# Layer 0's attention by pairs of query tiles, and the norms' inverse root as a power on GpSimd

## The chip, the cores and the metric

The kernel runs on one core of one Trainium2 chip. The core has five engines that run side by side, each with its own queue of instructions in a fixed order: TensorE (PE, matrix products and transposes, with a separate record for its weight loads, PEld), VectorE (DVE), ScalarE (ACT, table functions such as the exponential), GpSimd (POOL) and SyncE (SP, which here issues transfers). They meet through semaphores. TensorE writes into PSUM, eight banks of 128 partitions by 512 numbers in 32 bits; the other data lie in SBUF. The metric is the time on the device in microseconds (us) of one execution, the median of three runs.

## The reference

The input x is [4, 2048, 256] in 32-bit floats: 4 batches of 2048 positions. Two layers are computed, each as

```
xn = layernorm(x)                       # (x - mean) / sqrt(var + 1e-5), over 256
x  = x + mixer(xn) + second(xn)
```

In layer 0 the mixer is a gated linear recurrence along the 2048 positions (two 256x256 gates, then a scan). The second part is an attention of which, for every batch, the 4 most probable of 16 heads are chosen and scaled by gates:

```
dist = softmax(mean_over_positions(x @ Wr + br)); idx = top 4 of dist
Q, K, V = the chosen heads' projections, each [2048, 64], times the gate
attn = softmax(Q K^T / 8) over 2048 keys      # no mask
out  = concat(attn V) @ Wo + bo
```

In layer 1 the mixer is a causal attention with 16 heads of 16, and the second part is a channel mixing with sigmoid and squared relu. Layer 1 is not edited by the change, but its input is layer 0's x through the second norm, and the next batch's first norm is computed during its last part.

Note one property of the code below: the keys of a head are taken in the kernel as two halves of 1024 positions, so that 64-row operands of the two halves can lie in the two row halves of TensorE's array.

## The kernel before

For each batch the kernel does in turn: the first norm and its transposes (for batches after the first this runs beside the end of layer 1 of the batch before), the recurrence's gates and its scan, the choice of heads and the transfer of their weights, the projections of queries, keys and values, layer 0's attention (`attention0`), and layer 1 (`layer1`). The program is written as Python generators that are stepped at chosen places (`steps(stream, count)`), so that pieces of one stage stand in the queues between pieces of another. `in_order` (line 24) fixes that every engine runs its instructions in the order in which the program states them. So the order of the work is written out by hand, and an instruction that waits holds up all that stands behind it on its engine.

**The query tile.** `attention0` runs over the 4 chosen heads k and, for each, over 16 query tiles t of 128 positions. One tile goes through five steps of `Tile0`:

- `scores(j)`, lines 489 to 498, for two blocks j of 512 keys in each of two halves: two matmuls (line 494) with 64 rows each, one per row half of the array, into two banks, and a maximum over each bank on DVE (line 498). A tile has four score banks of 512 keys.
- `exponentials`, line 500: DVE takes the negative maximum `nm` over the four (line 502), and ACT makes four exponentials (line 508), each with its row sum, which appears in the profile as a second instruction, ACTIVATION_READ_ACCUMULATOR. The result is `p`.
- `turn(j)`, line 511: eight transposes of 128x128 (line 518) into two banks, which one DVE and one ACT copy (line 520) bring to `pT`.
- `weigh`, line 523: sixteen matmuls (line 528) of `pT` with the values, with 64 columns each, the two halves of the keys in the two column halves of the array, all accumulating in one bank `acc`; then ACT copies `o` (line 531), and DVE sums the row sums and inverts them, `rc` (lines 533 and 534).
- `project`, line 536: one matmul (line 538) of `o`, whose two halves of 64 rows are the two halves of the keys, with `wo2`, which holds the head's 64 rows of Wo twice; DVE multiplies by `rc` and adds to x (line 540).

A matmul in 32 bits leaves two records in the profile, a transpose one.

**The order in an iteration.** Four tiles are under way at a time. Iteration n states: the scores of the new tile, its exponentials, the projection of the tile three back, `turn(0)` of the last tile, `weigh` of the one before it, `turn(1)` of the last.

**The banks.** Scores have banks 0 to 3 to themselves. Everything else in `attention0` takes turns in banks 4 to 7 (`bank()`). Outside of `attention0` work takes turns in all eight (`own_bank()`), with a counter of its own.

**What stands between the tiles.** In each batch, `background` first finishes the recurrence: the bias is added to its result `y` for each of two halves (line 326, the second of these inside iteration 0), then eight steps, one a tile after tile 0, transpose four blocks of `y` (line 333) and add them to x on DVE (line 335). `rest_of_values` makes the last four value blocks in iteration 0 (lines 442 and 444). Before the head changes, `projecting` makes the next keys (lines 473 and 475) and, at every second head, the next queries (lines 456 and 457), one step a tile. In the last head, `norm.stats` takes the statistics of each finished tile (lines 253 and 254), and `all_blocks` norms each block of four tiles: the root on ACT (line 257), the inverse on DVE (line 261), four rows on DVE (line 268), and two times four transposes (line 274) with a copy by ACT (line 275). `opening` then starts layer 1's projections (lines 639 and 668) while the last tiles drain; layer 1 begins with its scores at line 712.

The first norm of each batch, in `prepared` (line 945), takes the root of all 16 tiles at once.

Of the kernel before, what the change touches and what calls it, by code (L numbers as in the profile page):

```python
# [10 lines left out]
FP = mybir.dt.float32  # L11
BF = mybir.dt.bfloat16
U32 = mybir.dt.uint32
AF = mybir.ActivationFunctionType
# [4 lines left out]
P = 128  # L19
QB = 512  # L20
# [52 lines left out]
def two_layers(ctx: ExitStack, tc: tile.TileContext, x, Wa, Wx, ba, bx, Lam,  # L73
# [36 lines left out]
    turn = {"high": 0, "all": 0}  # L110

    def bank():

        turn["high"] = (turn["high"] + 1) % 4
        return banks[4 + turn["high"]]

    def own_bank():

        turn["all"] = (turn["all"] + 1) % 8
        return banks[turn["all"]]  # L120
# [25 lines left out]
    eps_c = const.tile([P, 1], FP, tag="eps", name="eps_c")  # L146
    POOL.memset(eps_c, EPS)
# [94 lines left out]
    class Norm:  # L242
# [13 lines left out]
        def root(self, t, n):  # L256
            ACT.activation(self.rs[:, t:t + n], self.mv[:, t:t + n, 1:2].rearrange("p n o -> p (n o)"),
                           AF.Sqrt, bias=eps_c)

        def inverse(self, t, n):  # L260
            DVE.reciprocal(self.rs[:, t:t + n], self.rs[:, t:t + n])
# [217 lines left out]
    class Tile0:  # L479


        def __init__(self, b, k, t, qs, kT, v, xt):
            self.name = f"{b}_{k}_{t}"

            self.qT = [qs[(i + k) % 2] for i in range(2)]
            self.k, self.t, self.kT, self.v, self.xt = k, t, kT, v, xt
            self.p = []

        def scores(self, j):
            if j == 0:  # L490
                self.mx = sm.tile([P, 2 * NJ], FP, tag="mx0", name=f"mx0_{self.name}")
            for i in range(2):
                half_ = slice(i * DH, (i + 1) * DH)
                PE.matmul(banks[2 * j + i], lhsT=self.qT[i][half_, self.t * P:(self.t + 1) * P],  # L494
                          rhs=self.kT[half_, j * QB:(j + 1) * QB], start=True, stop=True)
            for i in range(2):
                n = 2 * j + i
                DVE.tensor_reduce(self.mx[:, n:n + 1], banks[n], AX.X, ALU.max)  # L498

        def exponentials(self):  # L500
            nm = sm.tile([P, 1], FP, tag="nm0", name=f"nm0_{self.name}")
            DVE.tensor_reduce(nm, self.mx, AX.X, ALU.max, negate=True)  # L502
            self.sums = sm.tile([P, 2 * NJ], FP, tag="sums", name=f"sums_{self.name}", bufs=4)
            for j in range(NJ):
                p = pex.tile([P, 2, QB], FP, tag="p", name=f"p0_{self.name}_{j}")
                for i in range(2):
                    n = 2 * j + i
                    ACT.activation(p[:, i, :], banks[n], AF.Exp, bias=nm, accum_out=self.sums[:, n:n + 1])  # L508
                self.p.append(p)

        def turn(self, j):

            if j == 0:
                self.pT = half_tile(f"pT_{self.name}").rearrange("p (n q) -> p n q", q=P)
            for i in range(2):
                tr = bank()
                for n in range(4):
                    PE.transpose(tr[:, n * P:(n + 1) * P], self.p[j][:, i, n * P:(n + 1) * P], ident)  # L518
                n0 = 8 * i + 4 * j
                (DVE.tensor_copy if i == 0 else ACT.copy)(self.pT[:, n0:n0 + 4, :],  # L520
                                                          tr.rearrange("p (n q) -> p n q", q=P))

        def weigh(self):
            acc = bank()
            N = NT // 2
            for n in range(N):
                for i in range(2):
                    PE.matmul(acc[i * DH:(i + 1) * DH, 0:P], lhsT=self.v[i][:, n, self.k * DH:(self.k + 1) * DH],  # L528
                              rhs=self.pT[:, 8 * i + n, :], start=(n == 0), stop=(n == N - 1))
            self.o = c1.tile([P, P], FP, tag="o", name=f"o_{self.name}")  # L530
            ACT.copy(self.o, acc[:, 0:P])
            self.rc = sm.tile([P, 1], FP, tag="rc", name=f"rc_{self.name}")
            DVE.tensor_reduce(self.rc, self.sums, AX.X, ALU.add)
            DVE.reciprocal(self.rc, self.rc)  # L534

        def project(self):
            ps = bank()
            PE.matmul(ps[:, 0:D], lhsT=self.o, rhs=wo2[:, self.k, :], start=True, stop=True)  # L538
            xs = rows_of(self.xt, self.t, 1)[:, 0, :]
            DVE.scalar_tensor_tensor(xs, ps[:, 0:D], self.rc, xs, ALU.mult, ALU.add)  # L540

    def attention0(b, xT, xt, ch, recurring, first, v, rest_of_values, norm, opening):


        qk, following = first, None
        background = recurring
        tiles = [None] * 3
        norming = iter(())

        def all_blocks():  # L550

            for q in range(NQ):
                norm.root(4 * q, 4)
                yield
                norm.inverse(4 * q, 4)
                norm.rows(q, 0, 2)
                yield
                yield
                norm.rows(q, 2, 4)
                yield  # L560
                for c in range(2):
                    norm.turn(q, c, ACT.copy)
                    yield
                    yield

        for n in range(NA * NT + 3):
            k, t = divmod(n, NT)
            if t == 0 and 0 < k < NA:
                steps(projecting, 100)
                qk = following  # L570
                following = None
            new = Tile0(b, k, t, *qk, v, xt) if k < NA else None
            last, second, third = tiles
            if t == NT - 6 and k + 1 < NA:
# [6 lines left out]
                projecting = concat(querying, keying)  # L581
            if new:
                new.scores(0)
                new.scores(1)
                if t >= NT - 6 and k + 1 < NA:
                    steps(projecting, 1)
                elif n >= (NA - 1) * NT + 7:
                    if n == (NA - 1) * NT + 7:
                        norming = all_blocks()
                    steps(norming, 1)  # L590
                new.exponentials()
                steps(rest_of_values, 4)
            else:
                steps(norming, 1)
            if n >= NA * NT:
                steps(opening, (1, 2, 1)[n - NA * NT])
            if third:
                third.project()
                if n - 3 >= (NA - 1) * NT:
                    norm.stats(n - 3 - (NA - 1) * NT)  # L600
            steps(norming, 1)
            steps(background, 1)
            if last:
                last.turn(0)
            if second:
                second.weigh()
            if last:
                last.turn(1)
            tiles = [new, last, second]
# [335 lines left out]
    def prepared(b, ready):  # L945
# [6 lines left out]
        def go():  # L952
# [4 lines left out]
            norm.root(0, NT)  # L957
            yield
# [76 lines left out]
```

## Time and profile before

The three runs took 4346.39, 4349.31 and 4352.74 us.

| | |
|---|---|
| median of the runs | 4349.31 us |
| the profiled execution | 4344.38 us |
| its span, first to last instruction | 4342.6 us |
| TensorE busy | 4249.8 us, 98% |
| VectorE busy | 3094.4 us, 71% |
| ScalarE busy | 2818.9 us, 65% |
| GpSimd busy | 1046.4 us, 24% |
| mean granted TensorE clock | 0.994 |
| first batch: first scores of layer 0 to first scores of layer 1 (lines 494 and 712) | 93.5 to 564.9 us |
| second batch: the same | 1168.1 to 1637.9 us |
| ScalarE's table loads for the roots (line 257) | 20, 25.7 us |

How to read it: a row of the timeline is start, duration, engine, line, operation, the tile written and the tiles read, and how many instructions were merged; what stands in brackets is the engine's idle time before it and what ended it. PE's busy time counts matmuls that overlap, so a busy PE isn't PE at its peak; the starts of its groups tell how long a group held it. In the table of stretches, a row has the stretch, its length, then busy time and count for PE, PEld, DVE, ACT and POOL, then PEclk, the granted clock as a part of full speed, and the transfers. Durations of single instructions overlap by some tens of nanoseconds where an engine works on several.

### The profile page before, as it was taken

Reading aid. Unit: us, or ns where it says so; the run is one execution under the profiler, and the core shown is the slowest. Engines: PE = TensorE matmul, PEld = TensorE weight load, DVE = VectorE, ACT = ScalarE, POOL = GpSimd, SP = SyncE. Lnnn points to the kernel's source line nnn. Section 1 sums busy time; section 2 is a strip of 40 time slices with the busy share of each in tenths; the row PEclk is TensorE's granted clock in tenths of the full one; section 3 lists DMA queues with packets and bytes.
Section 4 is the critical chain, followed back from the end, with each engine's and each line's share of the span. In section 5 each row is a group of like instructions: output and inputs, shape, how many; then the busy total and the mean of one; then the engine's idle time right before and its main releaser. Section 6 shows DMA issues by size and latency. Waiting matters only on the chain.

```text
span 4342.6 us, 86379 instructions
## 1 busy us (share of the span) xinstructions
PE 4249.8 (98%) x32994; PEld 2351.9 (54%) x32994; DVE 3094.4 (71%) x7292; ACT 2818.9 (65%) x6516; POOL 1046.4 (24%) x1322
## 2 busy tenths in 40 slices
PE   7999999999999999999999999999999999999999
PEld 4666653334566664333456676433446666643334
DVE  6666768887566677888656676888856667688882
ACT  4565648886555664888655566588765556558874
POOL 0000015544100001554410000255440000026544
PEclk9999999999999999999999999999999999999999
DMA  3000010100100000010000000011000000100000
GB/s 84 1 11 1 4 19 17 18 25 16 26 1 11 1 8 16 17 36 6 19 24 1 11 1 11 14 17 36 7 18 23 1 11 1 21 5 16 17 7 23
DMA packets 70818, 65.79 MB, mean 15 GB/s; under 512 B 37234, under 2 KB 58628, under 8 KB 68868
## 3 DMA queue, kind: packets, MB, share of 16 engines
q1 hardware_dynamic: 66624, 57.19, 6.1%
q8 instruction: 260, 4.26, 0.4%
q10 hardware_dynamic: 3780, 3.07, 0.2%
q14 instruction: 154, 1.26, 0.1%
HBM read 16.70 MB, written 8.39 MB: 6 GB/s over the span
## 4 chain that ended last, share of the span: by engine, by line
PE 90%; DVE 7%; ACT 1%; issue 1%; POOL 1%; DMA 1%; ACTq 0%; SPq 0%; POOLq 0%; DVEq 0%
PE bank L737 14%; PE bank L712 13%; PE bank L748 12%; PE bank L494 10%; PE bank L528 10%; PE bank L518 10%; PE bank L923 4%; PE bank L538 3%; DVE mx L498 3%; PE bank L639 3%; PE bank L290 3%; PE bank L473 1%; PE bank L456 1%; DVE mx L718 1%; PE bank L668 1%; PE bank L911 1%
## 5 line engine op out<-in xcount | busy, mean ns | idle before, releaser
L739 ACT ACTIVATE p<-bank 128x512 f32<-128x512 f32 (+3 forms) x2560 | 1183.0, 540 | 362.2 <-PE bank L737 258.4
L712 PE MATMUL bank<-k,q 32*128 32x512 f32 (+3 forms) x5120 | 1171.3, 577 | 1.8
L718 DVE TENSOR_REDUCE mx<-bank 128x1 f32<-128x512 f32 x1536 | 950.1, 681 | 200.5 <-PE bank L712 199.9
L737 PE MATMUL bank<-q,k 32*128 32x512 f32 (+3 forms) x5120 | 1073.4, 556 | 0.0
L508 ACT ACTIVATE p<-bank,nm 128x512 f32<-128x512 f32 x1024 | 689.2, 686 | 501.4 <-DVE nm L502 501.3
L755 POOL TENSOR_TENSOR o<-o,w 128x512 f32<-128x512 f32 (+3 forms) x576 | 627.4, 1089 | 794.7 <-ACT w L754 790.2
L498 DVE TENSOR_REDUCE mx<-bank 128x1 f32<-128x512 f32 x1024 | 635.8, 683 | 200.0 <-PE bank L494 199.8
L737 PEld LDWEIGHTS bank<-q,k 32*128 32x128 f32 x5120 | 422.0, 184 | 544.8 <-ACT p L739 409.1
L748 PE MATMUL bank<-p,v 128*17 128x512 f32 (+3 forms) x5120 | 601.5, 534 | 21.4 <-ACT p L739 14.3
L715 DVE CUSTOM_DVE_ANT_0 bank<-bank,cmask 128x128 f32<-128x128 f32 (+3 forms) x1024 | 472.5, 521 | 160.9 <-PE bank L712 105.6
L518 PE MATMUL bank<-ident,p 128*128 128x128 f32 x4096 | 549.8, 276 | 10.4 <-DVE x L335 5.1
L712 PEld LDWEIGHTS bank<-k,q 32*128 32x128 f32 x5120 | 459.7, 187 | 141.8 <-DVE mx L718 52.0
L520 DVE COPY pT<-bank 128x512 f32<-128x512 f32 x512 | 350.1, 684 | 248.6 <-PE bank L518 248.6
L494 PE MATMUL bank<-k,q 64*128 64x512 f32 x2048 | 514.5, 617 | 7.1 <-DVE v L444 7.1
L528 PE MATMUL bank<-pT,v 128*64 128x128 f32 x8192 | 503.8, 276 | 9.2 <-DVE x L540 8.5
L518 PEld LDWEIGHTS bank<-ident,p 128*128 128x128 f32 x4096 | 457.6, 141 | 82.0 <-DVE rc L534 22.6
L647 POOL MEMSET q<- 128x2048 f32 x16 | 29.6, 1848 | 1837.7 <-PE bank L528 1837.7
L528 PEld LDWEIGHTS bank<-pT,v 128*64 128x64 f32 x8192 | 441.9, 137 | 54.5 <-issue 34.8
L754 ACT COPY w<-bank 128x512 f32<-128x512 f32 (+3 forms) x576 | 305.3, 530 | 106.2 <-PE bank L748 85.2
L748 PEld LDWEIGHTS bank<-p,v 128*17 128x17 f32 x5120 | 88.8, 95 | 439.8 <-ACT p L739 237.2
L520 ACT COPY pT<-bank 128x512 f32<-128x512 f32 x512 | 309.7, 606 | 19.0 <-PE bank L518 17.7
L742 POOL TENSOR_SCALAR_AFFINE_SELECT p<-p 128x256 f32<-128x256 f32 x512 | 205.4, 413 | 385.4 <-ACT p L739 379.7
(164 smaller groups left out, 3495.3 us busy)
## 6 DMA issues: line engine op xcount, KB each, us to landing
x<-in_L_attn_x_dram SPq DMA_DIRECT2D x20, 512.0 KB
q<-q SPq DMA_DIRECT2D x64, 128.0 KB
vals<-o SPq DMA_DIRECT2D x256, 32.0 KB
out_dram<-x SPq DMA_DIRECT2D x32, 256.0 KB
q<-qp SPq DMA_DIRECT2D x48, 128.0 KB
k<-kp SPq DMA_DIRECT2D x48, 128.0 KB
q<-nmT SPq DMA_DIRECT2D x256, 2.0 KB
q<-qp SPq DMA_DIRECT2D x64, 32.0 KB
```

What stands on the lines that cost most here:

```text
L494: PE.matmul(banks[2 * j + i], lhsT=self.qT[i][half_, self.t * P:(self.t + 1) * P], rhs=self.kT[half_, j * QB:(j + 1) * QB], start=True, st ...
L498: DVE.tensor_reduce(self.mx[:, n:n + 1], banks[n], AX.X, ALU.max)
L508: ACT.activation(p[:, i, :], banks[n], AF.Exp, bias=nm, accum_out=self.sums[:, n:n + 1])
L518: PE.transpose(tr[:, n * P:(n + 1) * P], self.p[j][:, i, n * P:(n + 1) * P], ident)
L520: (DVE.tensor_copy if i == 0 else ACT.copy)(self.pT[:, n0:n0 + 4, :], tr.rearrange("p (n q) -> p n q", q=P))
L528: PE.matmul(acc[i * DH:(i + 1) * DH, 0:P], lhsT=self.v[i][:, n, self.k * DH:(self.k + 1) * DH], rhs=self.pT[:, 8 * i + n, :], start=(n == ...
L712: PE.matmul(s[:, 0:n], lhsT=self.qT[strip(h), self.qs], rhs=self.kT[strip(h), self.ks], start=True, stop=True)
L718: DVE.tensor_reduce(self.mx[:, h, :], s[:, 0:n], AX.X, ALU.max)
L737: PE.matmul(s[:, c0:QB], lhsT=self.kT[strip(h), self.ks], rhs=self.qT[strip(h), self.q0 + c0:self.q0 + QB], start=True, stop=True)
L739: ACT.activation(p[:, h % 2, c0:QB], s[:, c0:QB], AF.Exp, scale=SC1)
L748: PE.matmul(acc[32 * h:32 * h + DH1 + 1, c0:QB], lhsT=self.v[h], rhs=self.p[h // 2][:, h % 2, c0:QB], start=True, stop=True)
L755: POOL.tensor_tensor(self.o[:, c0:QB], self.o[:, c0:QB], w[:, c0:QB], ALU.add)
```

## The change

Layer 0's attention runs over pairs of query tiles, `Pair0`, 8 for a head, with a new order; and the norms no longer take a root on ACT.

- **Weighing and projection.** Both tiles of a pair are weighed together into bank 7, which nothing else in `attention0` uses: each tile has one column half of the array and goes through both halves of its keys. So `o` holds one tile in each 64 rows, it is copied once for the pair, and the projection is one matmul of 64 rows per tile, into two banks.
- **The order.** In an iteration stand: the late transposes of the second tile of the pair before, the projection of the pair before that, the first tile's scores and exponentials, half of the second tile's scores, half of the weighing, the other half of the scores, the other half of the weighing, and the first tile's transposes. The second tile's blocks are taken in the order 1, 0.
- **The banks.** `bank()` goes round banks 0 to 6, and shares its counter with `own_bank()`.
- **The steps between.** `background` and `projecting` are stepped at two places of an iteration, at its start and after the late transposes, both ahead of the first tile's scores; the norm's at four. `all_blocks` does the inverse and all four rows of a block at one step, at an iteration's end, and its first transposes at the next step.
- **The norms.** `root` goes. `inverse` adds eps on DVE and raises to the power -0.5 on GpSimd, with a tile that holds -0.5 as the exponent.

```diff
-    turn = {"high": 0, "all": 0}
+    turn = [0]
+
+    def own_bank():
+
+        turn[0] = (turn[0] + 1) % 8
+        return banks[turn[0]]
 
     def bank():
 
-        turn["high"] = (turn["high"] + 1) % 4
-        return banks[4 + turn["high"]]
...
+        if own_bank() is banks[7]:
+            own_bank()
+        return banks[turn[0]]
...
-        def root(self, t, n):
-            ACT.activation(self.rs[:, t:t + n], self.mv[:, t:t + n, 1:2].rearrange("p n o -> p (n o)"),
-                           AF.Sqrt, bias=eps_c)
-
         def inverse(self, t, n):
-            DVE.reciprocal(self.rs[:, t:t + n], self.rs[:, t:t + n])
+            rs = self.rs[:, t:t + n]
+            DVE.tensor_scalar(rs, self.mv[:, t:t + n, 1:2].rearrange("p n o -> p (n o)"), EPS, None, ALU.add)
+            POOL.tensor_tensor(rs, rs, minus_half[:, 0:n], ALU.pow)
...
+        def turn(self, j):
+
+            self.tr[j] = [bank() for _ in range(2)]
+            for i in range(2):
+                for n in range(4):
+                    PE.transpose(self.tr[j][i][:, n * P:(n + 1) * P], self.p[j][:, i, n * P:(n + 1) * P], ident)
+
+        def keep(self, j, i, copy):
...
+            copy(self.pT[:, n0:n0 + 4, :], self.tr[j][i].rearrange("p (n q) -> p n q", q=P))
+
+        def share(self):
+            self.rc = sm.tile([P, 1], FP, tag="rc", name=f"rc_{self.name}", bufs=6)
             DVE.tensor_reduce(self.rc, self.sums, AX.X, ALU.add)
             DVE.reciprocal(self.rc, self.rc)
...
+        def weigh(self, j):
+            acc, N = banks[7], NT // 4
+            for n in range(N):
+                for h in range(2):
+                    for i, tile_ in enumerate(self.tiles):
+                        PE.matmul(acc[i * DH:(i + 1) * DH, 0:P],
+                                  lhsT=self.v[h][:, N * j + n, self.k * DH:(self.k + 1) * DH],
+                                  rhs=tile_.pT[:, 8 * h + N * j + n, :], start=(j == n == h == 0),
+                                  stop=(j == h == 1 and n == N - 1))
+
+        def weighed(self):
+            self.o = c1.tile([P, P], FP, tag="o", name=f"o_{self.name}")
+            ACT.copy(self.o, banks[7][:, 0:P])
...
         def project(self):
...
+            self.ps = [bank() for _ in range(2)]
+            for i in range(2):
+                half_ = slice(i * DH, (i + 1) * DH)
+                PE.matmul(self.ps[i][:, 0:D], lhsT=self.o[half_, :], rhs=wo2[half_, self.k, :], start=True, stop=True)
...
             for q in range(NQ):
-                norm.root(4 * q, 4)
+                yield
+                yield
                 yield
                 norm.inverse(4 * q, 4)
                 norm.rows(q, 0, 2)
-                yield
-                yield
                 norm.rows(q, 2, 4)
                 yield
                 for c in range(2):
                     norm.turn(q, c, ACT.copy)
                     yield
-                    yield
+                yield
+                yield
...
+            steps(background, 1)
+            steps(projecting, 1)
+            steps(norming, 1)
+            if n >= NA * NP:
+                steps(opening, (2, 2)[n - NA * NP])
+            if before:
+                late = before.tiles[1]
+                late.turn(1)
+                late.turn(0)
+                late.keep(1, 0, DVE.tensor_copy)
+                late.keep(0, 0, DVE.tensor_copy)
+                late.keep(0, 1, ACT.copy)
+                late.keep(1, 1, ACT.copy)
+                for tile_ in before.tiles:
+                    tile_.share()
+            steps(background, 1)
+            steps(projecting, 1)
+            steps(norming, 1)
+            if older:
+                older.project()
+                older.add()
+                if n - 2 >= (NA - 1) * NP:
+                    for t in range(2):
+                        norm.stats(2 * (n - 2 - (NA - 1) * NP) + t)
             if new:
...
+                a.scores(0)
+                a.scores(1)
+                a.exponentials((0, 1))
                 steps(rest_of_values, 4)
...
             steps(norming, 1)
...
+            if new:
+                c.scores(1)
+            if n >= NA * NP:
+                steps(opening, 1)
+            if before:
+                before.weigh(0)
+            if new:
+                c.scores(0)
+                c.exponentials((1, 0))
+            if before:
+                before.weigh(1)
+            if new:
+                a.turn(1)
+                a.turn(0)
+                a.keep(1, 0, DVE.tensor_copy)
+                a.keep(0, 0, DVE.tensor_copy)
+                a.keep(1, 1, ACT.copy)
+            if before:
+                before.weighed()
+            if new:
+                a.keep(0, 1, ACT.copy)
+            steps(norming, 1)
+            older, before = before, new
...
-            norm.root(0, NT)
-            yield
             norm.inverse(0, NT)
```

## The prediction

> **What bounds the kernel now.** I read the page's busy shares and the chain that ended last, then the timeline of plain query tiles in layer 0, then the seams of that stage.
>
> ```profile
> PE 4249.8 (98%) x32994; PEld 2351.9 (54%) x32994; DVE 3094.4 (71%) x7292; ACT 2818.9 (65%) x6516; POOL 1046.4 (24%) x1322
> PE 90%; DVE 7%; ACT 1%; issue 1%; POOL 1%; DMA 1%; ACTq 0%; SPq 0%; POOLq 0%; DVEq 0%
> ```
>
> TensorE (PE) is busy and on the path nearly throughout; lines 494, 518, 528 and 538, layer 0's attention, hold a third of the chain. A gain must shorten PE's own row of work there. One plain tile:
>
> ```profile
> 356.83 1.99 PE L494 MATMUL bank<-k,q 64*128 64x512 f32 x8
> 357.99 2.48 DVE L498 TENSOR_REDUCE mx<-bank 128x1 f32<-128x512 f32 x4 [0.80 <-PE bank L494]
> 358.75 0.70 PE L538 MATMUL bank<-wo,o 128*128 128x256 f32 x2
> 359.29 1.04 PE L518 MATMUL bank<-ident,p 128*128 128x128 f32 x8
> 360.25 1.97 PE L528 MATMUL bank<-pT,v 128*64 128x128 f32 x32
> 360.51 0.16 DVE L502 TENSOR_REDUCE nm<-mx 128x1 f32<-128x4 f32 x1
> 360.58 0.47 DVE L540 SCALAR_TENSOR_TENSOR x<-bank,rc,x 128x256 f32<-128x256 f32 x1
> 360.76 0.69 ACT L508 ACTIVATE p<-bank,nm 128x512 f32<-128x512 f32 x1 [2.43 <-DVE nm L502]
> 360.97 0.68 DVE L520 COPY pT<-bank 128x512 f32<-128x512 f32 x1
> 361.35 0.19 ACT L508 ACTIVATION_READ_ACCUMULATOR p<-bank,nm 128x1 f32 x1
> 362.15 1.09 PE L518 MATMUL bank<-ident,p 128*128 128x128 f32 x8
> 363.17 1.99 PE L494 MATMUL bank<-k,q 64*128 64x512 f32 x8
> ```
>
> From scores to scores is 6.34 us: scores 1.92, projection 0.54, half the transposes 0.96, weighing 1.90, the other half 1.02. Inside a group matmuls start every 0.429 us (512 columns), 0.214 (256) or 0.108 (128), two at once where they lie in different row or column halves (the single records of L494 start in pairs 7 ns apart). So 4 x 0.429 + 2 x 0.214 + 16 x 0.108 + 16 x 0.108 = 5.62 us is streaming. The other 0.72 falls where the array's shape changes (128 rows to 64 rows, to 64 columns, and back): four changes a tile, 0.18 each. VectorE (DVE) needs some 4.5 us of the 6.34, ScalarE (ACT) 4.2. So PE alone sets the pace, and two tiles cost 12.68.
>
> **The pair, at PE's own pace.** Scores, transposes and weighing keep their matmuls (10.37 us a pair). The projection of two tiles was 4 x 0.214 = 0.86; now each tile's `o` fills one row half, two streams run at once, and it is 0.43. Changes of shape fall from eight to five (late transposes, projection and scores, weighing, scores, weighing, transposes): 5 x 0.18 = 0.90. Together 11.70 against 12.68. ACT also loses one 0.30 us copy of `o` a pair, off the path.
>
> **The wait that can eat it.** Seven banks now go round for everything. In the changed program's order, counting seven back: the last scores of the second tile reuse the bank of the first scores of the first tile, so PE waits there for that bank's exponential; weighing, transposes and the next pair stand behind. Let x be the start of the first tile's scores. PE reaches that matmul after 1.72 + 0.86 (six scores), 0.09 + 1.79 (half the weighing) and 0.10 for the change: x+4.56. The exponential: the late tile's second DVE copy starts at x-0.87 (its bank is whole 1.50 after the late transposes begin, x comes 2.37 after), takes 0.60, the four sum instructions 0.52, two additions 0.39 each (360.58 to 360.97): DVE is free at x+1.03, the first scores are readable at x+1.06. Maxima to `nm` 2.52 (357.99 to 360.51), to the exponential 0.25, its accumulator read 0.78 after its start, 0.05 to PE: x+4.66. PE waits 0.10. The other reuses come earlier than PE: the next pair's third scores wait for ACT's last late copy, some 0.15 us ahead. A pair takes 11.8: gain 0.88.
>
> **By stretch, each batch (32 pairs).**
> - Sixteen pairs with nothing beside them: 16 x 0.88 = 14.1.
> - Four with the next head's projections after the recurrence is over (tiles 8.06 and 8.21 before): PE's added work hides the wait: 3.9.
> - The first six pairs. Before, the recurrence's transposes come into the second tile. Now a step stands ahead of the first scores, and its transposes wait for `y`:
>
> ```profile
> 93.50 1.99 PE L494 MATMUL bank<-k,q 64*128 64x512 f32 x8
> 94.03 2.35 DVE L312 TENSOR_TENSOR_SCAN y<-at,y,bt 128x1024 f32<-128x1024 f32 x1
> 96.88 1.28 DVE L326 TENSOR_SCALAR y<-y,added 128x2048 f32<-128x2048 f32 x1
> ```
>
> PE is free at 93.5 and `y` is whole at 98.16: 4.7 us of idle PE. Then DVE does both L326 before the first maxima, the second tile's scores come after 7.1 us of values, and the transposes wait for its exponentials, so the second pair's scores start at 116.5 (third tile before: 108.35). The pairs after it take 12.8, 12.8, 12.3, 15.4, 11.8, against 14.25, 14.40, 14.41, 13.54, 16.42: tiles here took 7.20 because weighing waited for a bank held by L540. Sum: 0.2 us lost. In the second and fourth batch PE already idled to 1168.04 and 3312.03, `y` comes 1.1 later, and 3.4 is won.
> - The last six pairs, with the second norm. Two tiles' statistics (0.56 each, 527.10 to 527.66) stand before the maxima on DVE and push the exponential, and PE, by 1.1. Three times `inverse` and all four rows stand at the end of a pair with their transposes first in the next: copy to x+9.8, addition 0.15, power 0.3, hops 0.2, four rows of 0.34: done x+12.0, where PE arrived at x+9.4: 2.2 us of stall behind 0.43 of work. Three pairs of 12.85 and three of 15.9, 86.3 against 80.2: 6.1 lost.
> - The drain: the last block has the same stall, about 2.3, before had some 1.5 of stalls: 0.8 lost.
>
> Per batch 14.1 + 3.9 - 0.2 - 6.1 - 0.8 = 10.9, twice, and 14.5, twice: 50.8.
>
> **The norms.** Root, its table and the exponential's leave ACT, 39 of 58 table loads:
>
> ```profile
> 523.97 1.28 ACT L257 ACT_TABLE_LOAD   x1
> 525.26 0.30 ACT L257 ACTIVATE rs<-mv,eps_c 128x4 f32<-128x4 f32 x1
> 526.75 1.28 ACT L508 ACT_TABLE_LOAD   x1 [1.19 <-DVE nm L502]
> 528.05 0.69 ACT L508 ACTIVATE p<-bank,nm 128x512 f32<-128x512 f32 x1
> ```
>
> The next activation starts with the load's end, so a root costs 2.57 + 0.30. The Trainium skill (ScalarE: Activation LUTs, What ACT_TABLE_LOAD costs) adds a drain of 1.38 us to each switch; the row shows none, and I take the row: 39 x 1.28 = 50 us of ACT, by the page 104, nearly all beside PE. On the path I count 1 us in each of three layer-1 tails (by the page 2), where PE waits on ACT near 1043: 3. There `pow` stands behind a 1.1 us product on POOL, and DVE's rows move some 3 us, under a 4.65 us idle of DVE. The trace has no power on GpSimd (POOL). Nearest rows: 128x512 in 1270 ns and 128x128 in 453 extrapolate to 0.19 for four columns; above, I bound it by the 1.27 itself. I take 0.3, near the extrapolation; at 1.27, four exposed a batch cost 16 more. The last one stands behind two 1.85 us clearings of strips, whose buffers are free early: hidden by the last pair's weighing and six opening projections. At the start it runs under DVE's wait for L214: nothing.
>
> **The clock.** A new 4.7 us idle of PE stands in each batch.
>
> ```profile
> 3308.00:3312.00 4.00, 0.53 (x3) 0.13 (x1) 3.96 (x4) 0.00 (x0) 0.00 (x0) 1.00 0.00 0
> 3312.00:3324.00 12.00, 11.94 (x46) 8.13 (x48) 5.63 (x9) 5.13 (x11) 0.00 (x0) 0.86 0.00 1
> 1164.00:1168.00 4.00, 0.54 (x3) 0.14 (x1) 3.96 (x4) 0.00 (x0) 0.00 (x0) 1.00 0.00 0
> 1168.00:1180.00 12.00, 11.93 (x57) 8.45 (x58) 7.18 (x11) 5.03 (x11) 0.00 (x0) 1.00 0.01 2
> ```
>
> After PE's 3.5 us idle (second column of times) the clock column fell to 0.86 once of two, and that tile took 10.67 in place of 9.02: 1.65. The skill (TensorE: Matmul & The Clock Gate, The HAM clock gate) says one idle window of about 3.4 us halves the clock: four times 1.65, 5.0 more than now. By the rows, half the gaps: 1.6 more. I take 1.6.
>
> **Sum.** 50.8 + 3 - 1.6 = 52 off this execution's 4344.4 (span 4342.6 and 1.8 around it): 4292; the runs' median, 4349.3, lies 4.9 above it: **4297**.
>
> **Rivals.**
> - *Slower, by the bank wait.* Everything from the sums to the exponential is one chain behind one bank. The 52 us over some 116 pairs are 0.45 each: if the exponential releases the bank 5.1 us after x or later, nothing is left; at 5.4, 35 more are lost net, 4384. For it: latencies of 0.05 to 0.25 in a row, and DVE with 9 of 11.8 us filled. Against it: each link is a row, the slack to zero 0.45.
> - *The projection doesn't pair up, or the changes of shape stay.* 0.4 a pair comes back: 4343, within 0.2%. Against it: the paired starts of L494.
> - *Better.* PE waits nowhere in plain pairs (11.70), and DVE takes most of the norm's stalls: 4260 to 4275.
>
> **Numbers.** Forecast 0.62, its own range 4277 to 4320 (0.15 us a pair is 17; the power at its upper bound 16). Better 0.12; projection 0.10; bank wait 0.16. A measurement of this kernel tells 0.2% (8.7 us) from nothing. Faster 0.62 + 0.12 + half of 0.10 = 0.79; within 0.03; slower 0.18. The range takes in the better case and the projection, 4262 to 4345.
>
> **What would show it.** Plain pairs 11.8 from scores to scores; the two projection matmuls start together; PE's wait for the exponential in the last scores under 0.3; 4.7 us of idle before each batch's first transposes of `y`; a 2 us idle before three blocks of the norm; no root tables; `pow` near 0.3. Pairs above 12.3, or a power over 1.3, would make it wrong.

## The result, and the profile after

The changed kernel takes 4370.0 us (median of 5 runs, 4369.6 to 4372.3) against 4350.1 for the kernel before on the same chip: a ratio of 1.0048, 95% interval 1.0033 to 1.0062. It is slower by half a per cent, where 4297 and a gain were forecast. The profiled execution has a span of 4370.6 us against 4342.6.

The page of the kernel after, its busy shares and the chain that ended last:

```profile
PE 4219.6 (97%) x32994; PEld 2366.8 (54%) x32994; DVE 3127.8 (72%) x7292; ACT 2755.3 (63%) x6329; POOL 1072.1 (25%) x1342
PE 86%; issue 5%; DVE 5%; POOL 1%; ACT 1%; DMA 1%; ACTq 0%; SPq 0%; POOLq 0%; DVEq 0%
```

TensorE does the same work in 30 us less, and ScalarE has lost its tables, yet the span grew by 28: TensorE's share of the chain fell from 90 to 86%. Time went into not being busy. First the plain pair, in the timeline of the kernel after (start us, length us, engine, line, operation):

```profile
355.64 1.24 PE L493 MATMUL bank<-k,q 64*128 64x512 f32 x4
...
362.35 0.70 PE L553 MATMUL bank<-wo,o 64*128 64x256 f32 x4
...
362.89 2.74 PE L493 MATMUL bank<-k,q 64*128 64x512 f32 x12
...
366.75 0.69 ACT L507 ACTIVATE p<-bank,nm 128x512 f32<-128x512 f32 x1 [3.21 <-DVE nm L501]
...
367.46 1.24 PE L493 MATMUL bank<-k,q 64*128 64x512 f32 x4
```

From one last group of scores to the next (355.64 to 367.46) it is 11.82 us. The pair does what was forecast; the loss is elsewhere. The seam with the second norm shows most of it, in the same view (L693 is the clearing of a strip, which sets a buffer of layer 1's queries or keys to a constant):

```profile
523.39 0.16 DVE L259 TENSOR_SCALAR rs<-mv 128x4 f32<-128x4 f32 x1
...
523.63 1.01 POOL L260 TENSOR_TENSOR rs<-rs,minus_half 128x4 f32<-128x4 f32 x1 [29.87 <-DVE rs L259]
524.59 1.80 POOL L693 MEMSET q<- 128x2048 f32 x1
524.67 4.57 DVE L267 TENSOR_SCALAR xn<-x,mv,rs 128x256 f32<-128x256 f32 x4 [1.12 <-POOL rs L260]
526.33 1.80 POOL L693 MEMSET k<- 128x2048 f32 x1
...
528.42 1.35 PE L273 MATMUL bank<-ident,xn 128*128 128x128 f32 x4 [5.31 <-DVE xn L267]
...
529.56 3.31 PE L685 MATMUL bank<-xT,wq 128*128 128x512 f32 x4
...
532.71 1.88 PE L685 MATMUL bank<-xT,wk 128*128 128x512 f32 x4
...
550.54 4.83 DVE L267 TENSOR_SCALAR xn<-x,mv,rs 128x256 f32<-128x256 f32 x4 [1.12 <-POOL rs L260]
...
552.90 0.47 PE L273 MATMUL bank<-ident,xn 128*128 128x128 f32 x1 [3.76 <-DVE xn L267]
...
554.79 1.11 PE L273 MATMUL bank<-ident,xn 128*128 128x128 f32 x3 [1.41 <-DVE xn L267]
```

Three things are to be read here. The power takes 1.01 us, and VectorE waits 1.12 for it. The four rows of L267 take 4.57 us in place of some 1.4, exactly while GpSimd clears two strips. And after TensorE's idle of 5.31 us its next four matmuls take 3.31 us, where four of the same size take 1.88 a little later: half clock. At the last block (550.54) the rows meet two more clearings and take 4.83 us, and TensorE idles 3.76 and 1.41.

The windows view of the kernel after (stretch, its length, busy time and count on PE, PEld, DVE, ACT, POOL, then the granted clock) at a batch's start and at the norm's first block:

```profile
94.70:98.90 4.20, 0.00 (x0) 0.00 (x0) 4.16 (x4) 0.20 (x1) 0.00 (x0) 1.00 0.00 0
98.90:105.70 6.80, 6.27 (x16) 3.17 (x17) 4.96 (x8) 0.00 (x0) 0.00 (x0) 0.50 0.01 2
461.20:463.30 2.10, 0.00 (x0) 0.01 (x1) 0.97 (x4) 1.13 (x4) 1.01 (x1) 1.00 0.00 0
463.30:467.70 4.40, 4.38 (x20) 3.91 (x21) 1.96 (x5) 0.59 (x1) 0.00 (x0) 0.61 0.00 2
```

The second stretch is wholly at a clock of 0.50; in the fourth, 0.61 is the mean of 3.4 us at 0.50 (464.17 to 467.58 in the trace's clock record) and the rest at 1.00. In that record every batch has 27 us of it in layer 0, after five idles: 4.7 us before the transposes of `y`, 2.1 us at each of the first two blocks of the norm, 5.3 and 3.8 + 1.4 us at its last two.

Why the clearings run just then is in the waits (engine and line that waited, for whom, us in all, times, longest). Of the kernel before:

```profile
POOL q L647 <- PE bank L528: 1837.7, 8, 498.2
```

and of the kernel after:

```profile
POOL rs L260 <- DVE rs L259: 1936.1, 16, 431.9
```

Before, GpSimd stood at the clearings of layer 1's strips and ran them when their buffers came free. The rows of the norm were nearly or wholly done by then, and kept their 0.7 us for two (timeline of the kernel before):

```profile
500.63 0.73 DVE L268 TENSOR_SCALAR xn<-x,mv,rs 128x256 f32<-128x256 f32 x2
...
501.14 1.97 POOL L647 MEMSET q<- 128x2048 f32 x1 [498.18 <-PE bank L528]
...
507.43 0.70 DVE L268 TENSOR_SCALAR xn<-x,mv,rs 128x256 f32<-128x256 f32 x2
...
508.32 1.81 POOL L647 MEMSET k<- 128x2048 f32 x1 [5.21 <-PE bank L528]
```

Now GpSimd stands at the power. The clearings are queued behind it, their buffers are free by then (the view of the kernel after lists no wait of theirs), and they start the moment the power ends. That moment is also when VectorE's rows start.

### The profile page after: what moved, and what is told of

The parts are those of the page before. It is cut to its first block, busy times and chain, and to the rows that moved or that the text cites. A ratio compares the mean times of both kernels' runs of the same rounds, so it can differ in the third digit from the quotient of the medians.

```text
span 4370.6 us, 86287 instructions
## 1 busy us (share of the span) xinstructions
PE 4219.6 (97%) x32994; PEld 2366.8 (54%) x32994; DVE 3127.8 (72%) x7292; ACT 2755.3 (63%) x6329; POOL 1072.1 (25%) x1342
## 4 chain that ended last, share of the span: by engine, by line
PE 86%; issue 5%; DVE 5%; POOL 1%; ACT 1%; DMA 1%; ACTq 0%; SPq 0%; POOLq 0%; DVEq 0%
PE bank L783 14%; PE bank L758 14%; PE bank L794 12%; PE bank L493 10%; PE bank L515 10%; PE bank L540 10%; PE bank L969 4%; PE bank L289 3%; PE bank L685 2%; PE bank L553 1%; PE bank L714 1%; DVE mx L764 1%; PE bank L472 1%; PE bank L455 1%; PE bank L957 1%
## 5 line engine op out<-in xcount | busy, mean ns | idle before, releaser
L758 PEld LDWEIGHTS bank<-k,q 32*128 32x128 f32 x5120 | 471.6, 188 | 142.9 <-DVE mx L764 50.0
L493 PE MATMUL bank<-k,q 64*128 64x512 f32 x2048 | 543.2, 611 | 1.1 <-ACT p L507 0.3
L260 POOL TENSOR_TENSOR rs<-rs,minus_half 128x4 f32<-128x4 f32 (+1 forms) x20 | 27.9, 1393 | 1959.9 <-DVE rs L259 1936.1
L515 PE MATMUL bank<-ident,p 128*128 128x128 f32 x4096 | 496.3, 278 | 5.1 <-ACT p L507 5.0
L515 PEld LDWEIGHTS bank<-ident,p 128*128 128x128 f32 x4096 | 457.3, 144 | 48.6 <-issue 21.5
L521 ACT COPY pT<-bank 128x512 f32<-128x512 f32 x512 | 293.4, 600 | 75.1 <-PE bank L515 73.5
L493 PEld LDWEIGHTS bank<-k,q 64*128 64x128 f32 x2048 | 212.3, 188 | 169.9 <-issue 83.1
```

What stands on the lines that cost most here:

```text
L493: PE.matmul(self.s[j][i], lhsT=self.qT[i][half_, self.t * P:(self.t + 1) * P], rhs=self.kT[half_, j * QB:(j + 1) * QB], start=True, stop=True)
L515: PE.transpose(self.tr[j][i][:, n * P:(n + 1) * P], self.p[j][:, i, n * P:(n + 1) * P], ident)
L521: copy(self.pT[:, n0:n0 + 4, :], self.tr[j][i].rearrange("p (n q) -> p n q", q=P))
L758: PE.matmul(s[:, 0:n], lhsT=self.qT[strip(h), self.qs], rhs=self.kT[strip(h), self.ks], start=True, stop=True)
```

## The experiments

Times are medians; each ratio is to the kernel before on the same chip. "Stage" is the mean over four batches of the time from layer 0's first scores to layer 1's first scores, "half clock" the mean of it per batch at the granted clock of 0.5 in that stage and the 6 us ahead of it, both from the profiled execution.

| kernel | us | ratio (95%) | stage | half clock |
|---|---|---|---|---|
| before | 4350.1 | 1 | 470.9 | 0.9 |
| after | 4370.0 | 1.0048 (1.0033 to 1.0062) | 474.0 | 27.3 |
| 1 pairs, old norm | 4310.7 | 0.9914 (0.9901 to 0.9928) | 457.3 | 4.3 |
| 2 power, no pairs | 4388.7 | 1.0091 (1.0077 to 1.0105) | 479.8 | 6.0 |
| 3 idle filled by matmuls | 4345.4 | 0.9992 (0.9983 to 1.0000) | 467.4 | 3.4 |
| 4 `y` steps later | 4344.9 | 0.9991 (0.9982 to 0.9999) | 473.0 | 17.9 |
| 5 clearings on ScalarE | 4342.2 | 0.9987 (0.9981 to 0.9994) | 467.0 | 20.5 |
| 6 norm's steps apart | 4287.9 | 0.9863 (0.9849 to 0.9877) | 452.8 | 6.8 |
| 7 recut | 4235.1 | 0.9741 (0.9729 to 0.9754) | 444.9 | 0 |
| 8 = 1 and 4 | 4281.6 | 0.9848 (0.9835 to 0.9861) | 457.2 | 0 |
| 9 recut, old norm | 4254.2 | 0.9783 (0.9770 to 0.9796) | 450.4 | 0 |
| 10 = 2, clearings on ScalarE | 4371.6 | 1.0054 (1.0041 to 1.0068) | 475.0 | 1.7 |
| 11 idle filled by transposes | 4345.0 | 0.9993 (0.9985 to 1.0001) | 466.2 | 0.9 |

**Runs 1 and 2: one half of the change alone.** My first theory was that the pair's order brings the idles and the half clock behind them, and that the power is a side matter.

```diff
 # run 1, on the changed kernel: root and inverse as before; in all_blocks
                 yield
                 yield
+                norm.root(4 * q, 4)
                 yield
                 norm.inverse(4 * q, 4)
 # run 2, on the kernel before: inverse as in the changed kernel; in all_blocks
-                norm.root(4 * q, 4)
                 yield
                 norm.inverse(4 * q, 4)
```

> The pairs with the norm of before (root on ScalarE, inverse on VectorE; the root is issued where the second of three empty norming steps was). Theory 1 (new idles of TensorE, each followed by a stretch at half clock, lose what the pairs win): the idles come from where the steps stand in the pair, so they stay: 4360 to 4385 us, pairs of 11.8 us between, half clock again after each batch's first transposes of y and at the blocks of the second norm. Rival 2 (the power on GpSimd is what loses): the loss goes with it, 4335 or less.

> The kernel before with the norms' power on GpSimd, one query tile at a time as before. Theory 1: no new wait stands ahead of TensorE in this order, the root's tables leave ScalarE: 4335 to 4350. Rival 2 (the power loses): 4358 or more, with new idles of TensorE behind the rows of the norm.

Both fell on the rival's side. The pairs alone win 39 us; the power alone loses 39; on top of the pairs it loses 59. Run 2's timeline at the third block has the same picture in the old order:

```profile
530.34 1.01 POOL L259 TENSOR_TENSOR rs<-rs,minus_half 128x4 f32<-128x4 f32 x1 [27.28 <-DVE rs L258]
...
531.29 1.80 POOL L644 MEMSET q<- 128x2048 f32 x1
531.38 3.92 DVE L266 TENSOR_SCALAR xn<-x,mv,rs 128x256 f32<-128x256 f32 x2 [1.12 <-POOL rs L259]
...
533.03 1.81 POOL L644 MEMSET k<- 128x2048 f32 x1
...
535.96 1.12 PE L516 MATMUL bank<-ident,p 128*128 128x128 f32 x4 [4.69 <-DVE rc L531]
```

Two rows take 3.92 us there. VectorE's next work is the copies and sums of the tile, so TensorE idles 4.69 us at L516, where in the kernel before it idled 0.4. At the earlier blocks, with no clearing, that idle is 1.5.

In run 1 TensorE's idle at the norm is 1.2 us. It waits there for an exponential, which stands behind the root on ScalarE, and no half clock follows (timeline, then windows view of run 1, columns as above):

```profile
459.68 0.66 PE L517 MATMUL bank<-ident,p 128*128 128x128 f32 x4 [1.23 <-ACT p L509]
```

```profile
458.45:459.65 1.20, 0.00 (x0) 0.00 (x0) 0.99 (x3) 1.19 (x4) 0.00 (x0) 1.00 0.00 0
459.65:466.00 6.35, 6.29 (x41) 4.80 (x43) 4.65 (x15) 5.16 (x13) 0.00 (x0) 1.00 0.00 1
```

So the pairs alone don't bring the norm's half clock; the idle of 2.1 us that comes with the power does.

**Runs 3 and 11: the clock apart from the waits.** Work that serves nothing is put into TensorE's idle; every wait stays.

```diff
 # run 3, Norm.turn, with warm = 2, 2, 5, 4 for the first half of blocks 0 to 3
             ps = self.bank()
+            for _ in range(warm):
+                PE.matmul(ps, lhsT=ident, rhs=spread, start=True, stop=True)
 # run 3, recurrence, ahead of the first transposes of y
                 ps = bank()
+                for _ in range(5 if h == q == 0 else 0):
+                    PE.matmul(ps, lhsT=ident, rhs=spread, start=True, stop=True)
 # run 11: each such matmul becomes
+                for i in range(8):
+                    PE.transpose(ps[:, i % 4 * P:(i % 4 + 1) * P], spread[:, i % 4 * P:(i % 4 + 1) * P], ident)
```

> The changed kernel, every wait and step where it was, with matmuls of 512 columns that serve nothing ahead of the first transposes of y (5) and of the first transposes of each block of the second norm (2, 2, 5, 4), into the bank that those transposes overwrite. They fill TensorE's idle and finish no work. Theory 1 (the clock): the half-clock stretches at these places go; they are some 30 us a batch and stand partly on idle, so 9 to 13 us a batch come back: 4320 to 4335. Rival 3 (the waits themselves cost, the clock little): 4367 to 4374.

> The third run with idle filled by transposes (8 of 128 columns in place of each matmul of 512) of a constant, into the same banks. The norm's idle lies between two groups of transposes: 2.0 us before, 2.1 idle, 1.3 after. Theory 9 (the idle alone sets the clock back): transposes fill it as well as matmuls, the half-clock stretches go: 4340 to 4350 as in the third run. Rival 10 (for the clock transposes are idle time too, so that 2.1 us of idle are 5.4): the stretches at the norm stay: 4362 to 4378.

Both bring back 25 us. That is what the clock alone is worth, less than the 35 to 50 that I had put on it: run 3 fell outside its expectation. The first block in the timeline of the kernel after:

```profile
461.72 1.01 POOL L260 TENSOR_TENSOR rs<-rs,minus_half 128x4 f32<-128x4 f32 x1 [431.90 <-DVE rs L259]
462.76 1.38 DVE L267 TENSOR_SCALAR xn<-x,mv,rs 128x256 f32<-128x256 f32 x4 [1.13 <-POOL rs L260]
...
463.32 1.35 PE L273 MATMUL bank<-ident,xn 128*128 128x128 f32 x4 [2.12 <-DVE xn L267]
...
464.46 3.44 PE L515 MATMUL bank<-ident,p 128*128 128x128 f32 x16
```

and in that of run 3 (L273 is the filling, L519 the late tile's transposes):

```profile
457.89 1.88 PE L273 MATMUL bank<-spread,ident 128*128 128x512 f32 x4
460.09 1.30 PE L275 MATMUL bank<-ident,xn 128*128 128x128 f32 x4 [0.32 <-DVE xn L267]
461.22 1.91 PE L519 MATMUL bank<-ident,p 128*128 128x128 f32 x16
```

The norm's transposes wait for the same rows, but the sixteen transposes behind them take 1.91 us in place of 3.44. Run 11 settles a doubt: at the norm the idle lies between transposes, and if those counted as idle for the clock the gap would be some 5 us, not 2. Filled with transposes it keeps the clock just as well.

**Run 4: the start of a batch.**

```diff
+            if n > 0:
-            steps(background, 1)
+                steps(background, 1)
 # (both steps ahead of the scores), and
                 a.exponentials((0, 1))
+                if n == 0:
+                    steps(background, 1)
 ...
                 c.exponentials((1, 0))
+            if n == 0:
+                steps(background, 1)
```

> The changed kernel with the two steps of the recurrence that stand ahead of each batch's first scores moved: VectorE's addition behind the first tile's exponentials, the first transposes of y behind the second tile's scores. Removes the 4.7 us idle of TensorE. Theory 1 (idle and the half clock behind it): 4.7 us less 1 for a new wait, and 2 to 3 of clock, four times: 4342 to 4350. Rival 3 (the wait alone): 3 to 4 us four times, 4354 to 4358. Rival 4 (the first pair's values and exponentials set the pace there anyway): 4366 to 4371.

As theory 1 had it: 25 us come back, 6.3 a batch. In the profiled executions, which lie 26.5 us apart, 5.8 us come from between layer 1's last scores and the next batch's first (158.8 to 153.0), where the 4.7 us idle and the transposes stood, and 1.0 a batch from the stage.

**Run 5, and run 10 for the old order: the clearings.**

```diff
-            POOL.memset(t, (0.0, 1.0)[i])
+            if g < 2:
+                ACT.copy(t, (cmask, spread)[i][:, 0:1].to_broadcast([P, T]))
+            else:
+                POOL.memset(t, (0.0, 1.0)[i])
```

> The changed kernel with the clearing of the first four strips of layer 1 done by ScalarE (a copy of a constant column) in place of GpSimd's MEMSET; the power stays on GpSimd. Theory 5 (the power holds GpSimd's queue, so that the clearings run at the very time of VectorE's rows and slow them from 0.34 to some 1.2 us each): the last two blocks' rows are back at 1.4 us for four, TensorE's idles of 5.3 and 3.8 + 1.4 us fall to some 2.1 each, a half-clock window of 3.4 goes with each: 8 to 10 us a batch, 4328 to 4340. Rival (the rows are slow there for another reason): 4365 to 4373, rows unchanged.

> The kernel before with the power on GpSimd (as in the second run) and the first four clearings of a batch on ScalarE. Theory 5: the two rows that took 3.9 and 4.2 us are back at 0.7, the idle of 4.7 us and its half clock with them; what stays is the power's wait at each block (1.5 us of idle against 0.4 with the root): 5 to 7 us a batch of the 10 lost, 4360 to 4369. Rival (the power's latency is the whole loss): 4383 to 4390.

In run 5 28 us come back, just under the 30 to 42 expected. The timeline of run 5 at the block shown above:

```profile
522.80 1.01 POOL L260 TENSOR_TENSOR rs<-rs,minus_half 128x4 f32<-128x4 f32 x1 [29.86 <-DVE rs L259]
523.84 1.38 DVE L267 TENSOR_SCALAR xn<-x,mv,rs 128x256 f32<-128x256 f32 x4 [1.12 <-POOL rs L260]
...
524.40 1.35 PE L273 MATMUL bank<-ident,xn 128*128 128x128 f32 x4 [2.11 <-DVE xn L267]
...
526.27 1.90 ACT L694 COPY q<-cmask 128x2048 f32<-128x2048 f32 x1
```

The rows are back at 1.38 us and the idle at 2.11. In the groups of all rows of both norms (count, busy us, mean ns), after and run 5:

```profile
L267 DVE TENSOR_SCALAR xn<-x,mv,rs 128x256 f32<-128x256 f32 x128 | 78.4, 670 | 30.2 <-POOL rs L260 30.2
```

```profile
L267 DVE TENSOR_SCALAR xn<-x,mv,rs 128x256 f32<-128x256 f32 x128 | 52.4, 466 | 30.2 <-POOL rs L260 30.2
```

26 us of VectorE time; the idles that run 5 shortened (5.31 to 2.11, 3.76 + 1.41 to 2.05) are 6.3 us a batch, 25 in all, so nearly all of it was exposed. The time from the last pair's first scores to layer 1's falls from 63.0 to 56.0 us. Run 10 gave back 17 of the 39 us, less than expected: the two copies of 1.90 us stand in ScalarE's queue ahead of work that TensorE waits for, with a new idle of 1.81 us and, in two batches of four, half clock behind it. What stays of the loss in the old order I put down to the power's wait and to this; the two were not told apart.

**Runs 6 and 7: the steps set apart.** In run 6 only `all_blocks` changes; run 7 adds run 4, moves the norm's statistics behind the first tile's exponentials, and issues the second pair of clearings ahead of the last power.

```diff
 # run 6
             for q in range(NQ):
                 yield
                 yield
-                yield
                 norm.inverse(4 * q, 4)
+                yield
                 norm.rows(q, 0, 2)
+                yield
+                yield
                 norm.rows(q, 2, 4)
                 yield
-                for c in range(2):
-                    norm.turn(q, c, ACT.copy)
-                    yield
                 yield
-                yield
+                norm.turn(q, 0, ACT.copy)
+                yield
+                norm.turn(q, 1, ACT.copy)
 # run 7 besides: run 4, and
             if older:
                 older.project()
                 older.add()
-                (statistics of its two tiles)
 ...
                 steps(rest_of_values, 4)
+            if older and n - 2 >= (NA - 1) * NP:
+                for t in range(2):
+                    norm.stats(2 * (n - 2 - (NA - 1) * NP) + t)
 # and heads.open(1, 0), heads.open(1, 1) at n == NA * NP, ahead of older.project
```

> The changed kernel with only the steps of the second norm set apart: the power ahead of the second tile's scores, two rows at the pair's end, two rows ahead of the next projection, the transposes at that pair's end and at the start of the one after. Theory 1 and 5: the power is hidden, no transposes stand behind fresh rows; the pairs of 18.1 us fall to 13 to 14, the drain loses its idles: 12 to 17 us a batch, 4302 to 4322. Rival 6 (VectorE is full in these pairs, so the stall only moves to the wait for the exponentials): the pairs stay above 15.5, 4340 to 4360.

> All of it together: the recurrence's two steps behind the first tile's exponentials and the second tile's scores, the norm's steps set apart, its statistics behind the first tile's exponentials, and the second pair of clearings ahead of the last power in GpSimd's queue. If the losses add up as the single runs have them (6 us a batch at the start, 12 to 17 at the norm): 4270 to 4298, ahead of both kernels. If VectorE's or ScalarE's work sets the pace of the last six pairs: 4300 to 4330.

Both beat their expectation. Run 7's timeline at the first block:

```profile
445.89 0.17 DVE L259 TENSOR_SCALAR rs<-mv 128x4 f32<-128x4 f32 x1
...
446.14 1.01 POOL L260 TENSOR_TENSOR rs<-rs,minus_half 128x4 f32<-128x4 f32 x1 [416.50 <-DVE rs L259]
...
450.90 0.73 DVE L267 TENSOR_SCALAR xn<-x,mv,rs 128x256 f32<-128x256 f32 x2
...
453.46 0.72 DVE L267 TENSOR_SCALAR xn<-x,mv,rs 128x256 f32<-128x256 f32 x2
...
463.21 1.04 PE L273 MATMUL bank<-ident,xn 128*128 128x128 f32 x8
```

From the power's end to the rows are 3.75 us, from the last rows to their transposes 9.0: nobody waits. The power costs the same 1.01 us as before. In this kernel two rows still meet a clearing (3.71 us at 501.94), and it costs nothing visible, since their transposes come at 512.97. The last norm pairs, which took 12.87, 18.27, 12.77, 18.11, 12.77 us after, take 12.87, 12.87, 14.49, 12.87, 14.48 in run 6 and 11.89, 12.11, 13.41, 12.11, 13.41 in run 7. The difference between runs 6 and 7, 4.65 us a batch, I put down to the statistics' new place; it was not run alone. Run 7 is 2.6% faster than the kernel before.

**Runs 8 and 9: do the parts add, and is the power worth having?** Run 8 is run 1 with run 4's edit, run 9 is run 7 with the root on ScalarE where the power was and the inverse ahead of the first rows.

> The pairs with the norm of before (as in the first run) and the recurrence's two steps moved (as in the fourth). If the start of a batch and the norm are separate losses: 4310.7 less the 25 us that the move brought with the power in place: 4283 to 4291. If the half clock at the start matters less here: 4292 to 4300.

> The recut kernel with the norms' root on ScalarE and inverse on VectorE again, in the same steps (root where the power was, inverse ahead of the first two rows). Theory 7 (with its latency covered the power is worth having: a root is 1.28 + 0.30 + 1.28 us on ScalarE between the exponentials of the two tiles): 1.5 to 3 us in each of four pairs a batch, 4255 to 4285. Rival 8 (the power is worth nothing on TensorE's path wherever it stands): 4228 to 4240.

Run 8, slightly ahead of its expectation: 29 us less than run 1, so the start of a batch is a separate loss (25 with the power in place). Run 9 is 0.42% behind run 7, some 19 us, just under what theory 7 gave. Two pairs a batch take 13.96 us with the root where they take 12.11 with the power, 15 us in all, and the drain behind them takes 1.7 us a batch more. So the power is better than the root, once nothing waits for it.

## Why the prediction was wrong

*The pair: right.* Forecast 11.8 us, measured 11.82; the projection's matmuls run two at once (their records start 6 ns apart); the first pairs, forecast at 12.8, 12.8, 12.3, 15.4, 11.8, took 12.76, 13.00, 12.52, 15.67, 11.79. The projection of two tiles holds TensorE for 0.54 us (362.35 to 362.89), as long as that of one tile before. The bank wait, my slower rival, did not come: the last scores start 4.57 us after the first (362.89 to 367.46), where I had 4.56 without the wait and 4.66 with it.

*"The norms": the step that failed.* It took the root's removal as 3 us won, with a cheap power and with clearings that were hidden. Alone it lost 39 us (run 2). Three terms of it:
- "I take 0.3" for the power: 1.01 us, inside my bounds but near the upper one; the 128x16 form took 2.93 us. Four exposed waits a batch make 4 x 0.7 x 4 = 11 us as an estimate, if all of it is exposed.
- "The last one stands behind two 1.85 us clearings of strips, whose buffers are free early: hidden." I looked for the power waiting behind the clearings. It was the clearings that waited behind the power, and then ran on top of the rows: 9.40 us for eight rows at the last two blocks in place of 2.8. Run 5 prices it at 28 us, some clock included. The Trainium skill states a mechanism that would do it (SBUF — State Buffer, Who interferes with whom): VectorE and GpSimd share a pair of ports under an exclusive lock, held for a whole instruction, and a `tensor_scalar` can enter modes that need the pair. The trace agrees as to the wait: the first row's record began at 524.67, just after the first clearing, and ended at 528.28, just after the second (528.13); the next three took 0.40 each. At the last block, in three batches of four, one row came between the two clearings, and two rows took 2.3 and 2.0 us. In which mode the rows run, no run here shows. I counted the queue's order and not what would then overlap.
- "1 us in each of three layer-1 tails": not there. From layer 1's last scores to the next batch's first it was 156.0, 152.4 and 156.0 us before, and 156.6, 153.0 and 156.6 in run 2, which has the power and the old order: 0.6 longer.

*"The clock. I take 1.6."* By the two gaps of before I let half the idles of 4.7 us cost 1.65 each. In the changed kernel all four were followed by half clock, and so were the idles of 2.1 us at the norm, which I had counted as plain waits. Runs 3 and 11: 25 us.

*"Three times ... 2.2 us of stall ... pairs of 12.85 and 15.9"*: 12.87, but 18.1 to 18.3 in the first batch, 2.3 more. The idle was the size forecast (2.12) by luck. The terms I gave for the rows' end add up to x+11.8 and not x+12.0, and I let the transposes wait for all four rows; they start after the first row and then go at the rows' pace, 1.35 us where I had 0.43 (463.32). Idle and slow transposes together are 3.0 us, 0.8 above the 2.2, about what the power was dearer by. With the idle filled (run 3) these pairs take 16.65: the other 1.6 is the clock.

*"The drain: 0.8 lost"*: idles of 5.31 and 3.76 + 1.41 us by the collision, where 2.11 and 2.05 are left without it (run 5).

*The start of a batch*: 4.7 us of idle as forecast (4.73), first scores at 100.4, but the second pair's scores at 120.64 in place of 116.5, most of it half clock (with the idle filled, in run 3, 117.5).

The forecast left out 80 us of the profiled execution (4370.6 against 4290 forecast for its span). By cause, power 11, clearings 28 and clock 25 make 64, with some overlap between the last two. By place (starts of scores in the timelines), the last pair and the drain are the most. In the first batch the forecast for them comes to 52.0 us, from that pair's first scores to layer 1's: 15.9 for the pair, then the 35.3 of before and 0.8. They took 63.0, and 51.1 in run 1 with the root. Over the four batches they were 47 us over the forecast, the two stalled pairs 17, and the start of the batches, with the tails ahead of it, 14: 78 of the 80. With the idles filled (run 3) these three are 40, 6 and 4; with the clearings moved (run 5) the first is 19. My slower rival had 0.16 for a wait in the pair that never came. The one that came was in the norm, in a term costed at almost nothing.

## What to carry to other kernels

When an operation moves to an in-order engine that so far ran far ahead, ask what is queued behind it: those instructions are now tied to its input, and start together with its consumer. A producer, its consumer and TensorE's use of the result, issued back to back, expose every latency in the row; one step of other work between each pair hid a slower instruction wholly here. Price an idle of TensorE by the clock as well as by its length, and move work until it is under the length at which the clock falls (here few idles up to 1.6 us set it back, and most from 2.0 us on).

## What the runs showed of the hardware

- *How short an idle sets the clock back.* In the traces of both kernels and of runs 1 to 10 I took every idle of TensorE over 0.6 us after the start-up with no other within 12 us, and looked for half clock from its start to 3.6 us after its end. Up to 1.6 us: 4 of 151. From 2.0 to 2.3 us: 31 of 34. About 3.5 us: 3 of 6. From 4.7 us: 30 of 30. The Trainium skill's one idle window of about 3.4 us (TensorE: Matmul & The Clock Gate, The HAM clock gate) is too long for this case; the measurement decides. The three idles of 2.0 to 2.3 us without half clock are all in run 4. Why 3.5 us did less than 2.1 stays open.
- *Half clock here cost about a quarter of its length.* The 24 us a batch that run 3 removed were worth 6.2 us a batch (24.6 over four). Part of each stretch lies on idle that is there anyway: of the half clock from 525.61 to 532.44, 2.8 us.
- *A power of two tensors on GpSimd* takes 1.01 us for 128x4 and 2.93 for 128x16, far above what its products of 128x512 (1.27 us) suggest: by these two rows, some 0.16 us a column.
- *A root's tables cost 1.28 us each on ScalarE, and most of that costs nothing:* 20 roots bring 39 loads, 50 us of ScalarE, and with everything else covered they cost some 19 us more than the powers (run 9 against run 7).
